# Attention log weights in three bf16 parts, one row for each head and chunk, in a fused conv, scan, attention and router kernel

## The chip, the cores and the metric

The kernel runs on one core of a Trainium2 chip, as one launch. The metric is device microseconds of that core, the median of several runs. Five engines work beside one another: TensorE (PE; its weight loads are listed as PEld), VectorE (DVE), ScalarE (ACT), GpSimd (POOL) and the sync engine (SP), which here only issues DMAs.

## The reference, cut to what matters

The input is `x` of 16 batches, 128 channels and 64 x 64 positions, so 4096 tokens a batch. Layer 0 is a group norm and a gated state-space scan (a short causal convolution, 256 inner channels, 16 states). Layer 1 is a layer norm, an attention without queries per token, and a router with 64 experts. The change lies in the attention:

```python
s = jnp.einsum('hd,bthd->bth', q_proj, k)          # 8 heads, one score a token
m_A = jax.lax.cummax(s, axis=1)                    # running maximum over the tokens
exp_scores = jnp.exp(s - m_A)
u_A = jnp.cumsum(exp_scores, axis=1)               # running sum: the denominator
w_A = jnp.cumsum(exp_scores[..., None] * v, axis=1)
output = w_A / u_A[..., None]
```

So the weight of token t in the output at token T is exp((s - m)[t] - log u[T]) for t up to T. `(s - m)` is called the log weight below, and `log u` the log denominator.

## The kernel before, in words

A batch is worked through in 8 blocks of L = 512 tokens, and a block in 4 chunks of P = 128 tokens; there are 128 blocks. The main loop (lines 624 to 800) handles in one turn `k` the scan of block `k` (`cur`), the end of the scan of the block before (`prev`), the preparation of the next block (`nxt`), and the attention of block `m = k - 9`, whose last two chunks are finished one turn later (`mp_`); the layer norm of the next attention block is `mn`. Turns 9 to 127, 119 of them, hold scan and attention; the first 9 hold no attention, the last 10 no scan. A turn has 16 steps `n`, one for each state of the scan.

A step does, on DVE, `product` (bx = du times B, into PSUM), then what `beside(n)` puts there, then `scan` for each half of the channels, with `between(n)` between the two halves; POOL multiplies the result by C (`da<-h,bct`) and keeps the last state; PE adds it up one or two steps later (`add_y`, y_ps). ACT makes the decays (`da<-delta,a_neg`) up to 8 steps ahead. B and C come by a DMA (bct, 512 KB, five buffers) that SP issues 3 steps ahead. Every engine's instructions stay in the order in which the program calls them (`InOrder`), so the list by step in `beside` and `between` is the order on each queue, SP's too. All eight PSUM banks are in use; three of them ("ps") rotate over most of the products.

The attention of block m, by steps: keys (0 to 2), scores (`score`, 1 and 3), running maximum and log weight on DVE (`score_max`, step 4, rows 64u + 32q + g of a head, 512 tokens in a row), the exponential (`score_exp`, 5), the running sum (`score_sum`, between the scans of step 6), logarithm and inverse (`score_log`, 7), the transposed first weights for the carried state (`turn_weights`, 8), values (8, 9, and 3 of the next turn), the matrix of weights (`weights`: 12 and 13, and 4 of the next turn), the products with the values (`attend`: 13, 14, and 5 and 6 of the next turn) and the carried state (`carry_on`, DVE: 14, 15, and 6 and 7 of the next turn).

`weights` builds the exponents of four heads at a time as an outer sum in PSUM: a bf16 product of identity and causal mask, then one f32 product of `lh[u]` (log weights as rows, and a row of -1) with `rh` (rows of ones, and the log denominators). The rows that hold data are filled by small DMAs from SBUF to SBUF on the SP queue: 4 of `lh` after step 4 (`spread_weights`) and 4 of `rh` after step 8 (`spread_log`).

The layer norm of the next attention block runs in steps 10 to 12: centre on PE, square on ACT, variance on PE after the two dt products, logarithm and exponential on ACT, and on DVE the product xn (`ln_apply`).

Of the kernel before, what the change touches and what calls it, by code (L numbers as in the profile page):

```python
# [39 lines left out]
def conv_attn_hybrid(ctx: ExitStack, tc: tile.TileContext, x, w_in, conv_w, conv_b, w_xproj, w_dt, b_dt,  # L40
# [4 lines left out]
    NBLK = T // L  # L45
    NCH = T // P
# [33 lines left out]
    with ExitStack() as st:  # L80
# [33 lines left out]
        q1 = wp.tile([P, 4, 2, 32], F32, name="q1")  # L114
        e1 = wp.tile([P, L // P * 4, 2, 32], F32, name="e1")
# [4 lines left out]
        lh = [wp.tile([P, L], F32, name=f"lh{u}") for u in range(2)]  # L120
        rh = wp.tile([P, 4, L], F32, name="rh")
        carry = wp.tile([P, L // P, P], F32, name="carry")
        negc = wp.tile([P, 1], F32, name="negc")
        nc.vector.memset(negc, NEG)
# [3 lines left out]
        for u in range(2):  # L128
            nc.vector.memset(lh[u], 0.0)
            nc.vector.memset(lh[u][64 * u : 64 * u + 32, :], -1.0)  # L130
            nc.vector.tensor_scalar(lh[u][64 * u : 64 * u + 32, :], lh[u][64 * u : 64 * u + 32, :],
                                    ident[64 * u : 64 * u + 32, 64 * u + 4 : 64 * u + 5], None, ALU.mult)
        nc.vector.memset(rh, 0.0)
        for x in range(4):
            nc.vector.tensor_copy(rh[:, x, :], bc(ident[:, x : x + 1], [P, L]))
        for x in range(4):
            nc.vector.tensor_copy(rh[64:, x, :], bc(ident[64:, 64 + x : 65 + x], [64, L]))
# [11 lines left out]
        with tc.tile_pool(name="prep", bufs=1) as prep:  # L149
# [15 lines left out]
            for g in range(2):  # L165
                nc.vector.tensor_copy(q1[:, :, g, g], qt_ps[:, 4 * g : 4 * g + 4])
# [115 lines left out]
        def store_bc(k):  # L282

            w = blocks[k]
            w["bcs"] = bcd.tile([2 * N, L], F32, tag="bcs", name="bcs")
            SP.dma_start(w["bcs"], w["dbl"][R:, :])
# [171 lines left out]
        def score(m, g):  # L458

            s = att[m]  # L460
            if g == 0:
                s["s"] = acc.tile([P, L], F32, tag="acc", name="s_ps")
            for j in range(4):
                PE.matmul(s["s"][32 * j : 32 * j + 32, :], q1[:, j, g, :], s.pop(("kt", 4 * g + j)),
                          start=(g == 0), stop=(g == 1))

        def score_max(m):
            b, i = divmod(m, NBLK)
            s = att[m]
            if i == 0:  # L470
                gn[b]["mx"] = stp.tile([P, 1], F32, tag="mx0", name="mx0")
                gn[b]["den"] = stp.tile([P, 1], F32, tag="den0", name="den0")
            s["e"] = a1.tile([P, L], F32, tag="e", name="e", bufs=2)
            mx = s["mx"] = a1.tile([P, L], F32, tag="mx", name="mx")
            DVE.tensor_tensor_scan(mx, bc(negc, [P, L]), s["s"], NEG if i == 0 else gn[b]["mx"], ALU.max, ALU.max)
            DVE.tensor_copy(gn[b]["mx"], mx[:, L - 1 : L])
            DVE.tensor_tensor(s["e"], s["s"], mx, ALU.subtract)

        def spread_weights(m):
            s = att[m]  # L480
            for u in range(2):
                for q in range(2):
                    r = 64 * u + 32 * q
                    SP.dma_start(lh[u][64 * u + 2 * q : 64 * u + 2 * q + 2, :], s["e"][r : r + 2, :])

        def score_exp(m):
            s = att[m]
            s["w"] = short("w")
            ACT.activation(s["w"], s["e"], AF.Exp)

        def score_sum(m):
            b, i = divmod(m, NBLK)
            s = att[m]
            DVE.tensor_tensor_scan(s["mx"], bc(ones[:, 0:1], [P, L]), s["w"], 0.0 if i == 0 else gn[b]["den"],
                                   ALU.mult, ALU.add)
            DVE.tensor_copy(gn[b]["den"], s["mx"][:, L - 1 : L])

        def turn_weights(m):
            s = att[m]
            et = bank("et_ps")  # L500
            w = s.pop("w")
            for c in range(L // P):
                PE.transpose(et[:, bass.ts(c, P)], w[:, bass.ts(c, P)], ident)
            etv = et.rearrange("p (n q) -> p n q", q=32)[:, :, 0:2]
            ACT.copy(e1.rearrange("p n g q -> p n (g q)")[:, :, 0::33], etv)

        def score_log(m):
            s = att[m]
            ACT.activation(s["mx"], s["mx"], AF.Ln)

            ACT.activation(s["e"], s["mx"], AF.Exp, scale=-1.0)

        def spread_log(m):
            s = att[m]
            mx = s.pop("mx")
            for u in range(2):
                for q in range(2):
                    r = 64 * u + 32 * q
                    SP.dma_start(rh[64 * u + 4 : 64 * u + 5, 2 * q : 2 * q + 2, :], mx[r : r + 2, :])
# [49 lines left out]
        def attend_before(m, c):  # L569
            s = att[m]  # L570
            if m % NBLK or c:
                PE.matmul(s["o"][:, bass.ts(c % 2, P)], carry[:, (c - 1) % 4, :], s["e"][:, bass.ts(c, P)], start=False,
# [51 lines left out]
        for k in range(NK + LAG + 1):  # L624
# [10 lines left out]
            def between(n):  # L635

                if n == 6 and m is not None:
                    score_sum(m)
# [3 lines left out]
            def beside(n):  # L642
# [60 lines left out]
                if n == 7:  # L703
                    if mp_ is not None:
                        attend_before(mp_, 3)
                    if nxt is not None:
                        conv(nxt, 1)
                    decays(k, n, 2)
                    if m is not None:
                        score_log(m)  # L710
# [4 lines left out]
                if n == 8:  # L715
# [5 lines left out]
                    if nxt is not None:  # L721
                        xproj(nxt)
                    if m is not None:
                        value(m, 0, 1)
                if n == 9:
                    if cur is not None:
# [3 lines left out]
                if n == 10:  # L730
                    if mn is not None:
                        ln_center(mn)
                        ln_square(mn)
                    if nxt is not None:
                        delta(nxt)
                    if mn is not None:
                        ln_var(mn)
                    load_exp()
                if n == 11:
# [355 lines left out]
```

## Time and profile before

| what | value |
|---|---|
| median of 3 runs | 10953.4 us (10951.26 to 10953.72) |
| profiled execution, its own time | 10953.32 us |
| span of the profiled execution | 10951.6 us |
| PE busy in the span | 9913.9 us, 91% |
| DVE busy | 9289.6 us, 85% |
| ACT busy | 6992.7 us, 64% |
| POOL busy | 7051.2 us, 64% |
| DMA queue of SP | 47.6% of 16 engines' time |

The share of an engine is an average over stages: turns without attention (to about 640 us), turns with scan and attention (to about 9694 us), attention alone (to about 10110 us), and then the router, the experts and the last sum. A window of eight turns with both shows what limits the kernel for five sixths of its time. In the tables an entry such as `w_ps<-rh,lh` names what is written and what is read; a f32 product appears as two records. [...] successive starts, not durations, give its price.

### The profile page before, as it was taken

What the parts mean: (1) busy time and instruction counts of PE and PEld (TensorE: products, weight loads), DVE (VectorE), ACT (ScalarE), POOL (GpSimd) and SP (SyncE); (2) the same over time, 40 slices, a digit from 0 to 9 for tenths busy, and PEclk for the clock granted to TensorE, in tenths of its full rate; (3) what the DMA queues carried; (4) which work ended last, traced back from release to release, by engine and by line L of the source; (5) the groups of instructions that cost most, each with busy time, mean ns of one, the idle gap of its engine ahead of it and who ended that gap; (6) DMA issues with size and microseconds to landing.
All of it is one profiled execution on the core that took longest, in us unless ns stands there. A gap on an engine that the chain in (4) does not pass through costs nothing.

```text
span 10951.6 us, 152501 instructions
## 1 busy us (share of the span) xinstructions
PE 9913.9 (91%) x54748; PEld 6015.7 (55%) x54748; DVE 9289.6 (85%) x9757; ACT 6992.7 (64%) x11244; POOL 7051.2 (64%) x3871
## 2 busy tenths in 40 slices
PE   6689999999999999999999999999999999999775
PEld 4455555555555555555555555555555555555752
DVE  8999998989989998999999898899899988941743
ACT  4566666666666666666666676666666666655640
POOL 6877776777777777777777777777777777730000
PEclk7789999999999999999999999999999999999886
DMA  5554445444454545444454445444444444421358
GB/s 145 139 148 131 143 131 147 126 138 136 132 146 125 148 128 146 131 134 139 129 145 128 144 133 140 131 137 138 138 136 130 140 132 142 125 67 34 109 160 335
DMA packets 772553, 1502.42 MB, mean 137 GB/s; under 512 B 58240, under 2 KB 127504, under 8 KB 764624
## 3 DMA queue, kind: packets, MB, share of 16 engines
q1 hardware_dynamic: 769744, 1492.13, 47.6%
q8 instruction: 430, 7.05, 0.3%
q14 instruction: 331, 2.71, 0.1%
q10 hardware_dynamic: 2048, 0.53, 0.0%
HBM read 1361.89 MB, written 126.35 MB: 136 GB/s over the span
## 4 chain that ended last, share of the span: by engine, by line
PE 57%; DVE 18%; ACT 11%; issue 6%; POOL 4%; DMA 3%; SPq 0%; POOLq 0%; DVEq 0%; ACTq 0%
PE y_ps L31 11%; DVE h L31 10%; PE v_ps L31 8%; PE xs_ps L31 8%; PE w_ps L31 6%; PE ao_ps L31 5%; DVE bx L31 5%; PE o_ps L31 4%; POOL da L31 4%; PE k_ps L31 3%; PE dbl_ps L31 2%; PE z_ps L31 2%; PE s_ps L31 2%; DVE du L31 2%; PE carry_ps L31 1%
## 5 line engine op out<-in xcount | busy, mean ns | idle before, releaser
L31 POOL TENSOR_TENSOR da<-h,bct 128x1024 f32<-128x1024 f32 x2048 | 6508.1, 3178 | 2649.4 <-DVE h L31 2216.1
L31 DVE TENSOR_TENSOR_SCAN h<-da,state,bx 128x512 f32<-128x512 f32 x3584 | 4405.5, 1266 | 105.5 <-DVE bx L31 3.3
L31 DVE TENSOR_TENSOR bx<-du,bct 128x1024 f32<-128x1024 f32 x2048 | 2680.7, 1309 | 191.6 <-DMA bct<-bcs 125.4
L31 PEld LDWEIGHTS y_ps<-ident,da 128*128 128x128 f32 x16384 | 1983.0, 147 | 1364.1 <-issue 693.5
L31 PE MATMUL y_ps<-ident,da 128*128 128x128 f32 x16384 | 2249.6, 286 | 492.8 <-POOL da L31 492.7
L31 ACT ACTIVATE da<-delta,a_neg 128x512 f32<-128x512 f32 x4096 | 2582.2, 712 | 0.2
L31 ACT ACTIVATE kt<-k_ps 128x512 f32<-128x512 f32 x1024 | 586.0, 602 | 979.6 <-PE k_ps L31 979.6
L31 ACT ACTIVATE v<-v_ps 128x512 f32<-128x512 f32 x1024 | 611.5, 599 | 795.9 <-PE v_ps L31 795.8
L31 PE MATMUL w_ps<-rh,lh 128*128 128x512 f32 x2048 | 1051.8, 595 | 0.4 <-DMA rh<-mx 0.4
L31 PE MATMUL k_ps<-xn,wk 128*128 128x512 f32 x2048 | 1019.3, 634 | 0.0
L31 PEld LDWEIGHTS ao_ps<-wm,v 128*128 128x128 f32 x8192 | 965.9, 192 | 69.3 <-issue 69.3
L31 PE MATMUL ao_ps<-wm,v 128*128 128x128 f32 x8192 | 999.1, 275 | 0.0
L31 PE MATMUL v_ps<-wv,xn 128*128 128x512 f32 x2048 | 986.2, 605 | 2.9 <-ACT xc L31 2.6
L31 PE MATMUL xs_ps<-xb,wc 128*128 128x512 f32 x2048 | 925.8, 594 | 1.8 <-issue 1.8
L31 ACT ACTIVATE wm<-w_ps 128x512 f32<-128x512 f32 x1024 | 583.8, 591 | 220.0 <-PE w_ps L31 214.1
L31 PEld LDWEIGHTS v_ps<-wv,xn 128*128 128x128 f32 x2048 | 358.4, 189 | 519.4 <-issue 492.9
L31 POOL COPY state<-h 128x2 f32<-128x2 f32 x1792 | 636.7, 355 | 0.0
L31 PEld LDWEIGHTS k_ps<-xn,wk 128*128 128x128 f32 x2048 | 385.3, 203 | 452.1 <-issue 402.4
L31 DVE TENSOR_TENSOR_SCAN h<-da,bx 128x512 f32<-128x512 f32 x512 | 598.6, 1206 | 16.1 <-DVE carry L31 0.3
L31 PEld LDWEIGHTS xs_ps<-xb,wc 128*128 128x128 f32 x2048 | 370.6, 191 | 373.1 <-issue 373.1
L31 PEld LDWEIGHTS w_ps<-rh,lh 128*128 128x128 f32 x2048 | 393.1, 192 | 258.0 <-issue 225.0
L31 ACT ACT_TABLE_LOAD x395 | 506.8, 1283 | 12.9 <-PE v_ps L31 5.9
(170 smaller groups left out, 9602.8 us busy)
## 6 DMA issues: line engine op xcount, KB each, us to landing
bct<-bcs SPq DMA_DIRECT2D x2048, 512.0 KB
xs<-t_d SPq DMA_DIRECT2D x256, 256.0 KB
xs<-in_x_dram SPq DMA_DIRECT2D x128, 256.0 KB
xt<-in_x_dram SPq DMA_DIRECT2D x64, 512.0 KB
t_d<-xt SPq DMA_DIRECT2D x64, 512.0 KB
t_d<-xs SPq DMA_DIRECT2D x256, 128.0 KB
t<-t_d SPq DMA_DIRECT2D x128, 256.0 KB
tc<-t_d SPq DMA_DIRECT2D x16, 2048.0 KB
```

What stands on the lines that cost most here:

```text
L31: return lambda *args, **kw: self.tc.keep_in_program_order(f(*args, **kw))
```

## The change

Scores. Each chunk of each head gets a row of its own: `score` makes 16 products of 32 x 128 instead of 4 of 32 x 512 for each group, so a score tile has 128 columns, and rows 5g + c of each quadrant hold head group g, chunk c. Running maximum and sum scan 128 columns in each row, and `from_chunks` joins the four chunks of a head: a 32 x 32 block transpose on DVE of the last 32 columns, a copy of two numbers from the state of the block before (`zs`, two alternating tiles), two scans of 4 numbers, a transpose back. The log weight is then one scalar_tensor_tensor.

Log weight and log denominator lie beside each other in one tile (`x2`, 2 x 128 columns). ACT writes its bf16 rounding (first part), DVE the rest in two further bf16 parts (`split_more`, between the scans of step 8). The parts go to DRAM by one DMA (`store_parts`, after step 8) and come back by 16 DMAs of 3 rows each, 8 of `lh` and 8 of `rh` (`spread_parts`, after step 10). `lh` and `rh` are bf16, so the product in `weights` is bf16. The 8 small DMAs of before are gone. The running sum's logarithm takes the sum of the chunks before as bias; the inverse is made by four exponentials, one for each chunk, with a bias that switches the other rows off.

Order. The centre and square of the layer norm move from step 10 to the head of step 9, its variance ahead of the dt products, its logarithm and exponential from step 11 to 10, xn from step 12 to 13; `load_x(mn)` from step 8 to 7; `store_bc` from the SP queue to the ACT queue, right after xproj. `score_log` is called ahead of the decays of step 7.

```diff
+        q1 = wp.tile([P, 4, 2, CB, 32], F32, name="q1")
+        lh = [wp.tile([P, L], BF16, name=f"lh{u}") for u in range(2)]
+        rh = wp.tile([P, 4, L], BF16, name="rh")
...
-            SP.dma_start(w["bcs"], w["dbl"][R:, :])
+            ACT.dma_start(w["bcs"], w["dbl"][R:, :])
...
+            kt = [s.pop(("kt", 4 * g + j)) for j in range(4)]
+            for c in range(CB):
+                for j in range(4):
+                    PE.matmul(s["s"][32 * j : 32 * j + 32, :P], q1[:, j, g, c, :], kt[j][:, bass.ts(c, P)],
+                              start=(g == 0 and c == 0), stop=(g == 1 and c == CB - 1))
+
+        def from_chunks(m, what, local, first, op0, op1, data):
+            b, i = divmod(m, NBLK)
+            last = stp.tile([P, 32], F32, tag=f"last_{what}", name=f"last_{what}")
+            DVE.transpose(last, local[:, P - 32 :])
+            z = zs[what][m % 2]
+            if i == 0:
+                DVE.memset(z[:, 0:10:5], first)
+            else:
+                DVE.tensor_copy(z[:, 0:10:5], gn[b][what][:, 4:14:5])
+            gn[b][what] = z
+            for g in range(2):
+                DVE.tensor_tensor_scan(z[:, 5 * g + 1 : 5 * g + 5], bc(data[:, 0:1], [P, CB]),
+                                       last[:, 5 * g : 5 * g + 4], z[:, 5 * g : 5 * g + 1], op0, op1)
+            back = stp.tile([P, 32], F32, tag=f"back_{what}", name=f"back_{what}")
+            DVE.transpose(back, z)
+            return back[:, 31:32]
...
-            DVE.tensor_tensor_scan(mx, bc(negc, [P, L]), s["s"], NEG if i == 0 else gn[b]["mx"], ALU.max, ALU.max)
-            DVE.tensor_copy(gn[b]["mx"], mx[:, L - 1 : L])
-            DVE.tensor_tensor(s["e"], s["s"], mx, ALU.subtract)
+            DVE.tensor_tensor_scan(s["mx"], bc(negc, [P, P]), s["s"][:, :P], NEG, ALU.max, ALU.max)
+        def score_less(m):
+            before = from_chunks(m, "max", mx, NEG, ALU.max, ALU.max, negc)
+            DVE.scalar_tensor_tensor(x[:, 0, :], mx, before, s["s"][:, :P], ALU.max, ALU.subtract)
...
-            ACT.activation(s["w"], s["e"], AF.Exp)
+            ACT.activation(s["w"], s["x2"][:, 0, :], AF.Exp, scale=-1.0)
...
-            DVE.tensor_tensor_scan(s["mx"], bc(ones[:, 0:1], [P, L]), s["w"], 0.0 if i == 0 else gn[b]["den"],
-                                   ALU.mult, ALU.add)
-            DVE.tensor_copy(gn[b]["den"], s["mx"][:, L - 1 : L])
+            DVE.tensor_tensor_scan(s["sum"], bc(ones[:, 0:1], [P, P]), s["w"], 0.0, ALU.mult, ALU.add)
+            s["before"] = from_chunks(m, "sum", s["sum"], 0.0, ALU.mult, ALU.add, ones)
...
-            for c in range(L // P):
-                PE.transpose(et[:, bass.ts(c, P)], w[:, bass.ts(c, P)], ident)
+            PE.transpose(et[:, :P], s.pop("w"), ident)
+            for g in range(2):
+                ACT.copy(dst[:, :, :, g, 5 * g : 5 * g + 4],
+                         bc(src[:, 5 * g : 5 * g + 4, :].unsqueeze(3), [P, CB, 4, CB]))
...
-            ACT.activation(s["mx"], s["mx"], AF.Ln)
-            ACT.activation(s["e"], s["mx"], AF.Exp, scale=-1.0)
+            ACT.activation(x[:, 1, :], s.pop("sum"), AF.Ln, bias=s.pop("before"))
+            s["parts"] = a1.tile([P, 3, 2, P], BF16, tag="parts", name="parts")
+            ACT.copy(s["parts"][:, 0], x)
+        def inverse(m):
+            for c in range(CB):
+                ACT.activation(s["e"][:, c, :], s["x2"][:, 1, :], AF.Exp, bias=off[:, c : c + 1], scale=-1.0)
+        def split_more(m):
+            DVE.tensor_tensor(x, x, parts[:, 0], ALU.subtract)
+            DVE.tensor_copy(parts[:, 1], x)
+            DVE.tensor_tensor(parts[:, 2], x, parts[:, 1], ALU.subtract)
+        def store_parts(m):
+            s["pd"] = bcd.tile([P, 3, 2, P], BF16, tag="pd", name="pd")
+            SP.dma_start(s["pd"], s.pop("parts"))
+        def spread_parts(m):
             for u in range(2):
-                for q in range(2):
-                    r = 64 * u + 32 * q
-                    SP.dma_start(rh[64 * u + 4 : 64 * u + 5, 2 * q : 2 * q + 2, :], mx[r : r + 2, :])
+                for x in range(4):
+                    r = 64 * u + 32 * (x // 2) + 5 * (x % 2)
+                    SP.dma_start(lh[u][64 * u + 3 * x : 64 * u + 3 * x + 3, :].rearrange("t (c s) -> t c s", s=P),
+                                 pd[:, 0, r : r + CB, :])
+                    SP.dma_start(rh[64 * u + 12 : 64 * u + 15, x, :].rearrange("t (c s) -> t c s", s=P),
+                                 pd[:, 1, r : r + CB, :])
...
-                if n == 6 and m is not None:
-                    score_sum(m)
+                if m is not None:
+                    if n == 4:
+                        score_less(m)
+                    if n == 6:
+                        score_sum(m)
+                    if n == 8:
+                        split_more(m)
...
-                if n == 4 and m is not None:
-                    spread_weights(m)
...
                 if n == 8 and m is not None:
-                    spread_log(m)
-                if n == 8 and nxt is not None:
-                    store_bc(nxt)
+                    store_parts(m)
+                if n == 10 and m is not None:
+                    spread_parts(m)
```

The constant tiles are built differently too, once at the start: `lh` and `rh` hold -1 or +1 in the rows that no DMA fills, `off` is a small new constant, and `q1` has the form that the scores need.

## The prediction

> **What bounds the kernel now.** I read the page's busy line first, then a window of eight turns that hold both scan and attention, the waits in it, the order of single instructions in one turn, and the groups that the change touches.
>
> ```profile
> 4949.00:5558.00 609.00, 572.24 (x3147) 344.05 (x3147) 550.46 (x519) 413.00 (x650) 439.47 (x241) 0.98 0.48 136
> ```
>
> The columns are window, length, busy time of PE, PEld, DVE, ACT, POOL, then PE clock, DMA share, GB/s. A turn takes 609 / 8 = 76.1 us; the stretch from about 640 to 9694 us gives 9054 / 119 = 76.1 too. PE is busy 71.5 us of it, DVE 68.8, ACT 51.6, POOL 54.9. Two engines are near the bound, neither at it, so the waits decide.
>
> ```profile
> DVE xn L31 <- ACT rstd L31: 19.8, 8, 2.9
> DVE bx L31 <- DMA bct<-bcs: 10.0, 8, 1.8
> DVE xs L31 <- PE ao_ps L31: 7.0, 7, 1.1
> DVE carry L31 <- PE carry_ps L31: 6.7, 6, 1.6
> ```
>
> These are DVE's waits in that window: us, times, longest. Per turn 2.5 us for xn, 1.25 for the B and C transfer, 0.9 and 0.8 for products of PE, with small ones 46.7 / 8 = 5.8 us. So DVE waits for PE in steps 6 to 8, and in step 12 for a chain PE, ACT, DVE. The chain of waits says the same: in 5000 to 5200 us it lies on PE from step 1 to 10, then on ACT (square, table, delta, table, rstd) and then on DVE until POOL's last product.
>
> ```profile
> 5102.19 2.45 DVE L31 TENSOR_TENSOR_SCAN h<-da,state,bx 128x512 f32<-128x512 f32 x2
> 5105.68 2.62 DVE L31 TENSOR_TENSOR bx<-du,bct 128x1024 f32<-128x1024 f32 x1 [1.04 <-DMA bct<-bcs]
> 5110.74 0.69 DVE L31 TENSOR_TENSOR xn<-cen_ps,rstd 128x512 f32<-128x512 f32 x1 [2.44 <-ACT rstd L31]
> ```
>
> DVE in order of time, start and duration first: step 12. bx comes late, after POOL's product has begun (4.87), and takes 2.62 instead of 1.23 us. Then xn waits.
>
> ```profile
> 5070.77 0.38 PE L31 MATMUL w_ps<-maskb,identb 128*128 128x512 bf16 x1
> 5070.99 1.02 PE L31 MATMUL w_ps<-rh,lh 128*128 128x512 f32 x2
> 5071.85 0.38 PE L31 MATMUL w_ps<-maskb,identb 128*128 128x512 bf16 x1
> ```
>
> PE in order of time. By starts, a bf16 product of 512 columns costs 0.22 us and the f32 one 0.86.
>
> ```profile
> L31 DVE TENSOR_TENSOR_SCAN mx<-ones,den,w 128x512 f32<-128x512 f32 x112 | 195.9, 1749 | 0.0
> L31 DVE TENSOR_TENSOR_SCAN mx<-negc,mx,s_ps 128x512 f32<-128x512 f32 x112 | 142.6, 1273 | 65.8 <-PE s_ps L31 65.8
> L31 DVE TENSOR_TENSOR gs<-mv,gs 128x1 f32<-128x1 f32 x16 | 21.9, 1368 | 0.6
> L31 SPq DMA_DIRECT2D lh<-e x512: 562/575/702, 654.0 to 10076.0; - x171
> L31 SPq DMA_DIRECT2D bct<-bcs x2048: 355/360/2113, 42.7 to 9680.2; - x187
> ```
>
> Groups: busy us, mean ns (the SP rows: ns min/median/max). The same scan costs 0.48 us more with both inputs in SBUF, and a product of one element takes 1.37 us in the mean where it takes 0.16 alone: POOL holds them up. A small DMA of two rows occupies SP for 0.575 us, a large one for 0.36.
>
> [...]
>
> **The change, part by part (per turn).** I count DVE by starts. A plain step (bx, two scans) goes from 5058.30 to 5062.15: 3.85; 16 of them 61.6. On top: z 0.96, two xs 0.2, stats and du 1.9, xn 0.45, the carries about 0 (they fit in the gap before the scan), the maximum 1.75 (step 4: 5.60), the sum 1.45 or 2.10 (POOL in the way), mean 1.8. Sum 68.7; with 5.8 of waits and 1.4 of the doubled bx 75.9, against 76.1.
>
> DVE, removed: 1.75 + 1.8 = 3.55, leaving 65.15. Added:
> - Step 4. A scan of 128 columns, 1.27 / 4 plus a fixed part, so 0.38, half of it in the gap before the scan: 0.2. Then two transposes (0.155, the smallest instruction here, [...] I take 0.2), a copy 0.1, two scans of 4 numbers 0.19 and 0.15 (dependent tiny instructions start 0.19 apart in the group norm: 26.25, 26.44, 26.63), the last operation about 0.3 (the carry's 128x128 row: 0.28). 1.3 together. POOL's product still runs about 0.4 when the first two-input scan comes. 1.7.
> - Step 6. Scan 0.38, POOL in the way 0.75 (the 1.98 of one sum scan less 1.26), the rest as above without the last: 0.83. 1.95.
> - Step 8. Two products of 256 elements ([...]), a cast 0.25 (0.21 for 128 columns at the start of the trace) and gaps: 1.1, and 0.4 of POOL. 1.5.
>
> 65.15 + 5.15 = 70.3. Bounds: 1.2 less if POOL is never in the way and transposes cost 0.155; 2.5 more if every dependent instruction costs 0.35 and POOL 0.8 each time.
>
> PE, removed: 8 products, 0.86 to 0.22, 5.1 us; three of four transposes, 0.33. Added: 0.15 per score group (32 records of 32 x 128 at the carry's 0.57 per 16, 1.14 against 0.99), 0.3. So 71.5 falls to 66.3. Half of the 5.1 lies in steps 4 and 5, ahead of the carries and xs for which DVE waits; the other half in steps 12 and 13.
>
> Waits. xn: 2.5 now. Square before the gates and variance before dt bring rstd forward by about 2 us, xn itself is a step later: 0.3 left. A wait of about 1 us moves to the second dt product, which needs the bank of the first (as var waits now, 0.8). The transfer's 1.25 and the doubled bx 1.4 go, because SP no longer waits for dbl ahead of it (SP waits 31.0 us in the window for that): 0. xs and carries: PE comes 2.6 us earlier, DVE about as much since it doesn't wait any more; 0.6 and 0.5 left. At the turn of a batch 0.4.
>
> The sixteen DMAs. They stand on SP behind bct of step 13, which needs POOL's product of step 8. Counted from bx of step 8: split done at 4.6, parts stored by about 7 (at the start of the trace bcs is issued at 41.01 and the first bct, which waits for it, at 42.67: 1.7 us), bct issued at 9.4 to 9.8, 16 x 0.57 (three rows taken like two) = 9.1, so the last is issued at 18.9 and lands about 21. PE reaches weights(m, 0) at about 21.4: y of step 15 at 38, then 53.7 us of products, less 70.3. Behind it wait y of step 10, attend(0) and the carry that DVE wants at about 26.5; ready about 26.6. Behind the sixteen on SP stand xb and the bct of step 14, issued at 19.7; its 257 and 512 KB, at the 5.6 us that one needed behind two loads in step 12, land at about 25.3, wanted at 25.9. So the sixteen cost nothing up to 0.57 each, and nearly 16 times any excess. I put 0.5 of waits.
>
> ACT: exp, log, inverse and copy of 512 columns (0.62 + 0.62 + 0.63 + 0.22) give way to 0.31 + 0.31, four of 0.31, a copy 0.41, two of 0.25 and an issue of about 0.4 (as for o_d on ACT's queue): plus 1.1. It has 24 us free in a turn, which hide it; without that cover 1.1 x 119 = 131 us. POOL has no new work. load_x one step earlier costs nothing, its tile being free.
>
> Sum: 70.3 + 0.3 + 0.6 + 0.5 + 0.4 + 0.5 = 72.6. 76.1 - 72.6 = 3.5, times 119 = 416 us. The ten turns without scan: PE saves 5.1 of 44.1, but now nothing hides store, sixteen DMAs and landing (about 14 us from split to weights): 0, within 20 us either way. Turns without attention: 0. The start: about 1 us more of DVE constants. 10953.3 - 416 + 1 = 10538 us; the profiled execution stands 0.1 us from the median, so 10540.
>
> **Rivals.**
> 1. Slower: the sixteen DMAs become the bound. An issue above 0.82 us each uses up the gain (72.6 + 16 x 0.25 - 0.5 = 76.1); so would landings 4 us later. At 1.0 us, 79 us a turn and 11300. For it: they are all in one place, on one queue, between a late producer and two consumers with half a microsecond to spare; each has three rows of four pieces of 256 bytes. Against: nothing in the trace above 0.70 for a small DMA that didn't wait.
> 2. DVE becomes the bound at a higher price: small dependent instructions and POOL take 2.5 us more, 75.1 a turn, 10835. For it: the 1.37 us of a one-element product.
> 3. DVE's waits vanish altogether and small ones are cheap: 70 a turn, 10230. Against: PE at 66.3 plus its own waits is close behind.
> 4. No change: PE's relief is worthless because DVE's added work equals its waits. Needs 5.8 us more on DVE than removed; I find 1.6.
>
> **How the numbers follow.** Mine: 62%, 71.5 to 73.8 a turn, 10405 to 10680. Rival 2: 11%. Rival 3, all below 10405: 10%. Rival 1: 11% slower, and 3% where it eats most of the gain. Rival 4: 3%. A difference of 0.2%, 22 us, is about what a measurement can tell. Faster 0.62 + 0.11 + 0.10 + 0.03 = 0.86, same 0.03, slower 0.11. To hold 8 in 10 the range takes rival 2, the edge of 3 and the mild form of 1: 10380 to 10900.
>
> **What would show it.** w_ps as one bf16 record, PE busy near 66 a turn; xn's wait on rstd under 0.5; no bct wait in step 12; DVE near 70 with the scans of sum and the split stretched by POOL; `lh<-pd` near 0.57 each; no wait of w_ps on DMA. I am wrong if w_ps waits for `rh<-pd` by more than 2 us, if bx of step 14 waits for bct, or if the small DVE instructions sum to over 7 us.

## The result, and the profile after

The changed kernel takes 10682.4 us (median of 4 runs, 10670.12 to 10698.19); the kernel before, beside it on the same chip, 10953.6 us. The ratio is 0.9753, 95% interval 0.9736 to 0.977: 271 us, 2.5%, are gained. The prediction was 10540 within 10380 to 10900. The sign and the range are right; of the 416 us that the sum promised for the main stage, 249 came.

The profiled execution took 10670.12 us, its span is 10668.4 us. The main stage, from the first turn with attention to the last with a scan, went from 9060 us (647.1 to 9707.05) to 8811 us (643.9 to 9455.0): 74.0 us a turn in place of 76.1. The attention-only turns after it take 20 us less (402 to 382, to the last `xs`), the router and the experts behind them 11 us less, and the start 3 us less.

Eight turns with both scan and attention, the columns as in the window shown for before (window, length, busy PE, PEld, DVE, ACT, POOL, clock, DMA share, GB/s):

```profile
4798.10:5389.80 591.70, 541.56 (x3439) 336.32 (x3437) 553.26 (x609) 416.21 (x690) 436.00 (x242) 0.97 0.52 143
```

PE is busy 67.7 us a turn (71.5 before), DVE 69.2 (68.8), ACT 52.0 and POOL 54.5. DVE's waits in that window (us, times, longest):

```profile
DVE carry L31 <- PE carry_ps L31: 11.8, 7, 2.1
DVE xt L31 <- DMA xt<-in_x_dram: 6.8, 1, 6.8
DVE xn L31 <- ACT rstd L31: 3.4, 4, 1.1
DVE xs L31 <- PE ao_ps L31: 1.5, 2, 1.0
```

xn's wait fell from 2.5 to 0.43 us a turn, and the wait of bx for its transfer is gone. But the carry's wait rose from 0.8 to 1.5, and a wait for the residual input (`xt<-in_x_dram`) has grown from 0.2 to 6.8 us, in one place: the turn with the residual.

What the carry waits for, in one turn. First ACT, then PE, in order of time (start, duration):

```profile
4921.76 2.55 ACT L31 ACTIVATE da<-delta,a_neg 128x512 f32<-128x512 f32 x4
4924.21 1.06 ACT L31 ACTIVATE wm<-w_ps 128x512 f32<-128x512 f32 x2
```

```profile
4917.00 1.46 PE L31 MATMUL dt_ps<-dbl,wdt 8*128 8x512 f32 x2 [0.78 <-ACT delta L31]
4918.39 3.25 PE L31 MATMUL y_ps<-ident,da 128*128 128x128 f32 x16
...
4921.69 0.38 PE L31 MATMUL w_ps<-rh,lh 128*128 128x512 bf16 x1
...
4924.84 0.38 PE L31 MATMUL w_ps<-maskb,identb 128*128 128x512 bf16 x1 [1.03 <-ACT wm L31]
4925.27 1.95 PE L31 MATMUL ao_ps<-wm,v 128*128 128x128 f32 x16
4927.15 0.65 PE L31 MATMUL carry_ps<-v,e 128*32 128x128 f32 x16
```

The bf16 product makes exponents ready at about 4922. ACT, in its written order, does four decays first and takes the exponential only at 4924.2. PE stands for 1.03 us until a bank is free, and the products behind it, the carry's among them, come later. The 16 products of y_ps ahead of the weights took 3.25 us, where 16 of the same took 1.97 at 4931.37: the granted clock of TensorE was 0.83 from 4915 to 4919 us, 0.74 from 4919 to 4923 and 1.00 in the next 4 us. More on that below.

Before, the wait between PE and ACT ran mostly the other way: ACT waited for the f32 products. The same pair over the whole span, of before and then of after:

```profile
ACT wm L31 <- PE w_ps L31: 214.1, 444, 3.5
```

```profile
ACT wm L31 <- PE w_ps L31: 46.6, 39, 8.2
...
PE w_ps L31 <- ACT wm L31: 161.2, 215, 1.6
```

The groups that the change touches (busy us, mean ns | idle before it; SP rows: ns min/median/max):

```profile
L31 PE MATMUL w_ps<-rh,lh 128*128 128x512 bf16 x1024 | 410.3, 401 | 52.3 <-DMA rh<-pd 52.0
L31 DVE TENSOR_TENSOR bx<-du,bct 128x1024 f32<-128x1024 f32 x2048 | 2524.5, 1233 | 72.8 <-DMA bct<-bcs 2.7
L31 DVE TENSOR_TENSOR_SCAN sum<-ones,w 128x128 f32<-128x128 f32 x128 | 144.6, 1130 | 0.0
L31 DVE TENSOR_TENSOR x<-x,parts 128x256 f32<-128x256 f32 x128 | 102.3, 799 | 0.5
```

```profile
L31 SPq DMA_DIRECT2D lh<-pd x1024: 232/276/1077, 676.7 to 9812.7; - x171
```

`w_ps<-rh,lh` is one bf16 record. bx has its plain 1.233 us again (1.309 in the mean before). The sum's scan (1.13 us in the mean) and the first operation of the split (0.80) are stretched: with POOL's product out of the way they took 0.42 and 0.40 (at 4755.99 and 4767.91, in the kernel with PE's cost back, see below). A small DMA occupies SP for 0.276 us, not 0.57.

### The profile page after: what moved, and what is told of

It reads as the page before. It is cut to its first block, busy times and chain, and to the rows that moved or that the text cites. A ratio compares the mean times of both kernels' runs of the same rounds, so it can differ in the third digit from the quotient of the medians.

```text
span 10668.4 us, 165082 instructions
## 1 busy us (share of the span) xinstructions
PE 9433.2 (88%) x59484; PEld 5912.8 (55%) x59484; DVE 9296.3 (87%) x11184; ACT 7034.1 (66%) x11884; POOL 6977.9 (65%) x3875
## 4 chain that ended last, share of the span: by engine, by line
PE 56%; DVE 16%; ACT 15%; issue 5%; POOL 4%; DMA 4%; SPq 1%; POOLq 0%; ACTq 0%; DVEq 0%
PE y_ps L31 10%; DVE h L31 8%; PE v_ps L31 8%; PE xs_ps L31 7%; PE ao_ps L31 7%; PE k_ps L31 4%; POOL da L31 4%; PE o_ps L31 4%; DVE bx L31 3%; ACT L208 2%; PE dt_ps L31 2%; ACT da L31 2%; PE carry_ps L31 2%; PE dbl_ps L31 2%; PE w_ps L31 2%
## 5 line engine op out<-in xcount | busy, mean ns | idle before, releaser
L31 POOL TENSOR_TENSOR da<-h,bct 128x1024 f32<-128x1024 f32 x2048 | 6597.9, 3222 | 2470.7 <-DVE h L31 1524.4
L31 DVE TENSOR_TENSOR_SCAN h<-da,state,bx 128x512 f32<-128x512 f32 x3584 | 4424.3, 1266 | 101.5 <-DVE bx L31 2.8
L31 PEld LDWEIGHTS y_ps<-ident,da 128*128 128x128 f32 x16384 | 2057.4, 152 | 1318.9 <-POOL da L31 652.6
L31 PE MATMUL y_ps<-ident,da 128*128 128x128 f32 x16384 | 2347.5, 294 | 485.3 <-POOL da L31 485.1
L31 ACT ACTIVATE da<-delta,a_neg 128x512 f32<-128x512 f32 x4096 | 2606.8, 722 | 0.2
L31 DVE TENSOR_TENSOR bx<-du,bct 128x1024 f32<-128x1024 f32 x2048 | 2524.5, 1233 | 72.8 <-DMA bct<-bcs 2.7
L31 ACT ACTIVATE kt<-k_ps 128x512 f32<-128x512 f32 x1024 | 586.6, 602 | 862.8 <-PE k_ps L31 858.1
L31 ACT ACTIVATE v<-v_ps 128x512 f32<-128x512 f32 x1024 | 611.6, 599 | 795.3 <-PE v_ps L31 795.2
L31 PE MATMUL k_ps<-xn,wk 128*128 128x512 f32 x2048 | 1047.1, 648 | 0.0
L31 PE MATMUL v_ps<-wv,xn 128*128 128x512 f32 x2048 | 1000.2, 611 | 6.3 <-ACT xc L31 6.0
L31 PE MATMUL ao_ps<-wm,v 128*128 128x128 f32 x8192 | 1003.1, 276 | 0.0
L31 PEld LDWEIGHTS ao_ps<-wm,v 128*128 128x128 f32 x8192 | 971.2, 193 | 25.6 <-issue 6.2
L31 PE MATMUL xs_ps<-xb,wc 128*128 128x512 f32 x2048 | 924.3, 594 | 1.8 <-issue 1.8
L31 DVE TENSOR_TENSOR_SCAN h<-da,bx 128x512 f32<-128x512 f32 x512 | 601.2, 1207 | 15.4 <-DVE bx L31 0.5
L31 PEld LDWEIGHTS v_ps<-wv,xn 128*128 128x128 f32 x2048 | 338.7, 189 | 475.0 <-issue 308.7
L31 PEld LDWEIGHTS k_ps<-xn,wk 128*128 128x128 f32 x2048 | 389.9, 206 | 377.4 <-issue 346.5
L31 PE MATMUL w_ps<-maskb,identb 128*128 128x512 bf16 x1024 | 411.5, 402 | 187.4 <-ACT wm L31 161.2
L31 PEld LDWEIGHTS xs_ps<-xb,wc 128*128 128x128 f32 x2048 | 370.0, 191 | 372.1 <-issue 372.1
L31 ACT ACTIVATE wm<-w_ps 128x512 f32<-128x512 f32 x1024 | 539.4, 594 | 48.2 <-PE w_ps L31 46.6
L31 POOL COPY state<-h 128x2 f32<-128x2 f32 x1792 | 472.8, 264 | 0.0
L31 PE MATMUL w_ps<-rh,lh 128*128 128x512 bf16 x1024 | 410.3, 401 | 52.3 <-DMA rh<-pd 52.0
```

The costliest lines, as they stand in the source:

```text
L31: return lambda *args, **kw: self.tc.keep_in_program_order(f(*args, **kw))
```

## The experiments

The theory to which the runs led: DVE's work plus DVE's waits add up to the time, but don't set it; PE and what PE waits for set the pace of the turn, so PE's 5 us are the gain, and two waits that the new schedule made (ACT's exponential behind the decays, the residual behind the sixteen DMAs) take part of it back. It was not the theory at the start: of the first four expectations, those for the order alone and the rows alone still count DVE's waits as gains, that for the run without the split calls DVE the bound, and all four, PE's cost back among them, missed with their own ranges. The rivals: the order of the layer norm and of the store of B and C is the gain; DVE's added work is what took the rest; the sixteen DMAs did.

All ratios are against the kernel before, run beside the kernel. The differences in us below are of medians; taken by the ratios they change by about 8 us at most.

| kernel | us | ratio, 95% |
|---|---|---|
| after | 10682.4 | 0.9753 (0.9736 to 0.977) |
| before + new order alone | 11023.1 | 1.0072 (1.0057 to 1.0087) |
| new rows and parts, old order | 10781.0 | 0.985 (0.9836 to 0.9865) |
| after + PE's cost back | 11092.5 | 1.0131 (1.0114 to 1.0148) |
| after, no split on DVE | 10662.9 | 0.9739 (0.9724 to 0.9753) |
| before + store of B and C on ACT | 10949.0 | 0.9992 (0.9984 to 1.0001) |
| after + decays a step later | 10533.3 | 0.9622 (0.9607 to 0.9636) |
| after + residual earlier | 10609.4 | 0.9691 (0.9677 to 0.9706) |
| after + both | 10455.1 | 0.9553 (0.9537 to 0.9569) |
| both, no split on DVE | 10427.7 | 0.9522 (0.9507 to 0.9536) |
| after, each small DMA twice | 11820.9 | 1.0799 (1.0783 to 1.0815) |
| after + sixteen other small DMAs | 10928.1 | 0.9977 (0.9968 to 0.9985) |

### Order alone, and rows alone

The kernel before with only the moves of the order (f32 rows and products as they were):

```diff
                 if n == 9:
+                    if mn is not None:
+                        ln_center(mn)
+                        ln_square(mn)
...
                 if n == 10:
-                    if mn is not None:
-                        ln_center(mn)
-                        ln_square(mn)
+                    if mn is not None:
+                        ln_var(mn)
                     if nxt is not None:
                         delta(nxt)
-                    if mn is not None:
-                        ln_var(mn)
                     load_exp()
-                if n == 11:
                     if mn is not None:
                         ln_scale(mn)
                 if n == 12:
-                    if mn is not None:
-                        ln_apply(mn)
                     if m is not None:
                         weights(m, 0)
                 if n == 13:
+                    if mn is not None:
+                        ln_apply(mn)
...
-            SP.dma_start(w["bcs"], w["dbl"][R:, :])
+            ACT.dma_start(w["bcs"], w["dbl"][R:, :])
```

(`store_bc` right after xproj, and `load_x(mn)` in step 7, belong to it.) The second kernel is the changed one with these edits taken back.

> The kernel before with the moves of order alone: the layer norm's centre and square at the head of step 9, variance ahead of dt, xn in step 13, load_x in step 7, bcs issued on ACT's queue; scores, log weights and the f32 product in weights stay as they were. My theory (PE's products and the order each had to go): DVE loses its waits for rstd (2.5 us a turn), for bct (1.25) and the doubled bx (1.4), but PE still has 71.5 us of work and its waits, so a turn falls from 76.1 to about 74.5: 10760 us, between 10690 and 10850. Rival A (the order is the whole gain): a turn of 74.1 and 10680 within 30. Rival B (PE's shorter product is the whole gain): 10950 within 30.

> The changed kernel with the old order: rows of a head and a chunk, three bf16 parts and the bf16 product, but the layer norm in steps 10 to 12 as before, load_x in step 8, bcs on SP after step 8 (behind the store of the parts). My theory: DVE's waits for PE in steps 6 to 8 go (1.7 us a turn), those for rstd and bct stay (5.1), and DVE's own work is 1.6 more: about 76 a turn, 10940 us, between 10850 and 11020. Rival A (the order is the whole gain): the same or slower, 10950 to 11150, since only DVE's added work is left. Rival B (the product is the whole gain): 10700 within 40.

Order alone: 11023.1, slower by 0.7%; rows alone: 10781.0. All the numbers expected for the two missed, those of the rivals too. DVE's waits with the order alone:

```profile
DVE carry L31 <- PE carry_ps L31: 710.9, 327, 10.8
DVE xn L31 <- ACT rstd L31: 346.4, 122, 9.7
```

Before, the carry waited 271.9 us in all and xn 387.3. The wait of bx for its transfer is all but gone here too (5.3 us left of 125.4), and it bought nothing: 439 us more of waiting stand at the carry. Read as a square, by the ratios and 10953 us: the rows alone give 0.0150, or 164 us; with f32 rows the new order costs 0.0072, or 79 us, and with bf16 rows it gains 0.985 - 0.9753, or 106 us. The order only pays once PE has become shorter. So "the order is the gain" falls, and so does a sum in which each part has a value of its own.

PE itself became slower with the order alone. Busy time and number of instructions, of before and then with the order alone:

```profile
PE 9913.9 (91%) x54748; PEld 6015.7 (55%) x54748; DVE 9289.6 (85%) x9757; ACT 6992.7 (64%) x11244; POOL 7051.2 (64%) x3871
PE 10058.7 (91%) x54748; PEld 6074.6 (55%) x54748; DVE 9102.6 (83%) x9757; ACT 6994.6 (63%) x11244; POOL 6998.0 (63%) x3871
```

The same products kept PE busy for 145 us more, and the mean granted clock fell from 0.948 to 0.939. Much of it lies behind the layer norm's products: in the 10 us from the first dt product of a turn the clock was 0.95 in the mean of 118 turns before, 0.87 with the order alone and 0.86 in the changed kernel. The store of B and C alone (below) left PE's busy time at 9908.6 and the clock at 0.949, so the slower PE came with the moves of the layer norm and of `load_x`. How much of the 79 us this makes up, and what lowers the clock there, no run shows.

### PE's cost back, and DVE's cost of the split away

To the changed kernel, three products with a zero weight for each product of `weights` give PE back what bf16 saved, in cost and not in value:

```diff
+                for _ in range(3):
+                    PE.matmul(rp, zero, rh[:, :, bass.ts(c, P)], start=False, stop=False)
                 PE.matmul(rp, lh[u][:, bass.ts(c, P)], rh[:, :, bass.ts(c, P)],
                           start=False, stop=True)
```

The other kernel leaves out the split on DVE in step 8 (second and third part are zeros):

```diff
-                    if n == 8:
-                        split_more(m)
```

> The changed kernel with PE's saving given back and nothing else: each bf16 product in weights is followed in the same sum by three more of the same shape with an all-zero weight matrix, so four bf16 products take the time of the f32 one (4 x 0.22 us against 0.86), the sum is unchanged, and PE has 5.1 us more a turn. My theory: PE is then at 71.5 plus 3 us of waits, a turn at 75.5 to 76.5: 10850 to 10970 us. Rival A (PE had slack all along): within 40 us of 10682.

> The changed kernel without the split on DVE: the second and third parts stay zero, so the log weights and log denominators are only bf16 precise; the 17 DMAs and all else stay. It takes 1.7 us of DVE a turn away (0.80 + 0.29 + 0.43 and gaps, of which 0.4 to 0.6 is POOL in the way). My theory (DVE is the bound now, PE close behind): DVE would gain 1.7 but PE lets it have only part, about 0.8 a turn: 10590 us, between 10500 and 10650. Rival (PE, not DVE, is the bound now, as the carry's wait in step 14 suggests): within 40 us of 10682.

PE's cost back: 11092.5, 410 us over the changed kernel, or 3.45 us a turn for some 5.1 us of PE (24 products of 0.21 us by starts). It is slower than before, and beyond the 10850 to 10970 that were expected. It differs from the order alone only by the rows and parts, at the same busy time of PE (10062.1 us and 10058.7), and is 0.6% slower. So the change, put together in this order, has three parts: the order costs 0.7% of the time of before, the rows and parts with their DMAs 0.6%, and the shorter product on PE gains 3.8%.

DVE's split away: 10662.9, 20 us for 1.7 us a turn of DVE, which would be 200 us if DVE set the pace. The expected 10500 to 10650 was missed; the rival's number, within 40 us of the changed kernel, came. DVE's waits without the split:

```profile
DVE carry L31 <- PE carry_ps L31: 359.5, 144, 15.2
DVE xn L31 <- ACT rstd L31: 279.9, 119, 11.3
```

xn waited 118.1 us in the changed kernel: 162 of the 200 us became waiting for the layer norm. Time that DVE saves there turns into a wait. PE's time counts at about two thirds (3.45 of 5.1).

### The store of B and C on ACT's queue, alone

```diff
-            SP.dma_start(w["bcs"], w["dbl"][R:, :])
+            ACT.dma_start(w["bcs"], w["dbl"][R:, :])
```

(called right after xproj instead of after step 8; the kernel before otherwise)

> The kernel before with one edit: the store of B and C goes from SP's queue (after step 8) to ACT's queue, right after xproj. If PE sets the pace, the 1.25 us a turn that bx of step 12 waits for the transfer, and the 1.4 us by which POOL doubles its time, move to other waits of DVE (xn, carries), and the time stays: 10910 to 10960. Rival, my prediction's sum, in which DVE's time and waits add up to the turn: 1.25 to 2.65 us a turn, 10630 to 10800.

10949.0, a ratio of 0.9992: no change, as the theory of PE had it. DVE lost most of its wait for the transfer (125.4 us in all, 18.0 left) and 136 us of work, the doubled bx (9289.6 to 9153.5 us). What it waits for now:

```profile
DVE xn L31 <- ACT rstd L31: 629.6, 126, 11.9
DVE carry L31 <- PE carry_ps L31: 273.1, 131, 10.8
```

xn waits 242 us more than before. In the prediction this edit was counted as 1.25 + 1.4 us a turn.

### The two new waits removed

Decays of the next steps start one step later, so that ACT takes the exponential of `weights(m, 0)` first; the residual's four loads are issued four steps earlier, ahead of the sixteen DMAs on SP:

```diff
-                    if 4 <= n <= 6 or n >= 11:
+                    if 4 <= n <= 6 or n >= 12:
```

```diff
-                if 8 <= n <= 11 and i == 1 and cur is not None:
-                    load_residual(b, n - 8)
+                if 4 <= n <= 7 and i == 1 and cur is not None:
+                    load_residual(b, n - 4)
```

> The changed kernel with one call of decays fewer: those of step 11 move to the steps 12 to 15, so that ACT takes up the exponential of the weights of chunk 0 right after rstd instead of behind four decays (2.55 us). My theory of the carry's wait in step 14 (1.45 to 2.1 us in every turn): PE's fourth mask product waits 1.0 to 1.6 us for a bank that ACT empties late, because the product is now shorter than ACT's exponential and ACT stands behind the decays. Then the wait of w_ps on ACT wm goes, the carry's falls below 0.8, and about 1 us a turn is won: 10570 us, between 10520 and 10640. Rival (the carry is late because PE reaches step 12 late, its dt product waiting for delta): w_ps no longer waits but the carry still does by over 1.2, within 40 us of 10682.

> The changed kernel with the four loads of a batch's residual issued after steps 4 to 7 of its second turn instead of 8 to 11, ahead of the sixteen small DMAs. In the window of eight turns DVE waits 6.8 us for xt once (0.2 before the change), in a turn of 77 to 78 us. My theory (the last part of the residual stands on SP behind the sixteen): the wait goes, these 15 or 16 turns fall by 4 to 6 us, 10610 us, between 10580 and 10640. Rival (the 2 MB themselves take that time, whenever they are issued, and hold up bct): 10682 within 25.

> The two edits together, on the changed kernel: decays of step 11 later, residual loads after steps 4 to 7. They touch different waits, so their gains should add: about 10500 us, between 10440 and 10590. If only one of them holds, 10570 to 10610.

10533.3 (149 us less), 10609.4 (73 less), and both 10455.1 (227 less; the sum of the two is 222), each within its expected range. With both, ordinary turns went from about 72 to 74 us to about 70.5 to 72, and the turn with the residual from about 77.6 to 73. DVE's and PE's waits with the decays a step later:

```profile
DVE carry L31 <- PE carry_ps L31: 237.3, 99, 14.6
```

```profile
PE w_ps L31 <- ACT wm L31: 63.5, 128, 1.3
```

PE's wait for ACT's exponential fell from 161.2 to 63.5 us, the carry's from 360.7 to 237.3 (between 1000 and 9000 us, where every turn has scan and attention, from 158.8 to 46.4). Part of the gain shows in PE itself: for the same number of products its busy time fell from 9433.2 us to 9366.4 with the decays later and to 9315.9 with both, at a mean granted clock of 0.931, 0.934 and 0.941. The runs don't part this from the waits. The version with both leaves none of the work out; it is 2.1% faster than the changed kernel, 4.5% faster than the one before.

> The kernel with both repairs (decays a step later, residual four steps earlier) and without DVE's three operations of the split in step 8: the second and third part are zeros, so 1.7 us a turn of DVE's work are left out. In the kernel after leaving them out was worth 20 us. If the repairs have made DVE the bound, it is worth most of 1.7 x 119 = 200 us now: 10455 less 120 to 200, 10255 to 10335. If PE still sets the pace, within 40 us of 10455. Between: both, 10335 to 10415.

With both repairs and without the split (the edit shown above): 10427.7, 27 us less than 10455.1. That is within the 40 us expected if PE still sets the pace, so DVE's operations in step 8 are still not on the path. Only that place was tried; nothing here says what DVE's time is worth in other steps.

### The price of the small DMAs

First each of the sixteen DMAs was issued twice; then sixteen more went behind the sixteen, to a tile that nobody reads:

```diff
+            for y in range(16):
+                SP.dma_start(spare[8 * y : 8 * y + 3, :].rearrange("t (c s) -> t c s", s=P), pd[:, 0, y : y + CB - 1, :])
```

> The changed kernel with each of the sixteen small DMAs issued twice, the same bytes to the same place: 32, at 0.28 us each (measured median) 5 us more of SP in steps 10 to 12. My prediction said that the sixteen cost nothing up to a threshold and then nearly their excess: with the last issued at 17.7 us after bx of step 8 and needed by PE at 22, some 2 us are free, so 2 to 3 us a turn are lost, in the waits of w_ps for rh<-pd and in the carry: 10990 us, between 10880 and 11100. Rival (the landings are hidden well beyond that): within 40 us of 10682.

> The kernel after, with sixteen more small DMAs from the stored parts into a tile that nobody reads (three rows of three pieces of 256 bytes each), issued behind the sixteen in pairs with them, ahead of what stands behind them on SP. No data is changed. A clean price of a longer burst, since no two neighbours have one destination. By the kernel after an issue takes 0.276 us: 16 more are 4.4 us, so xb and the transfer of step 14 are issued 4.4 us later (22.1 us after bx of step 8 in place of 17.7) and land at about 27.7, wanted at 25.9. My prediction's threshold (slack about 0.5 us at a last issue of 18.9, so about 1.7 us at 17.7) then charges 4.4 - 1.7 = 2.7 us a turn, some part of it taken back by waits that are there anyway: 10682 + 119 x (1.5 to 2.7), 10860 to 11000, and bx waits for bct by 1.5 to 2.7 us a turn. Rival: the burst is hidden with far more room than I saw; then within 40 us of 10682 and no bct wait.

Twice: 11820.9, 1138 us or 9.6 a turn, far above what was expected. It is no clean price: SP issued four and then stood for about 1 us, again and again, and its own waits name the landing of the first DMA to the same place, 8 times a turn:

```profile
SPq L31 <- DMA lh<-pd: 1084.5, 1024, 4.9
```

This wait is not among those of the changed kernel. The run also shows who stands behind a late burst:

```profile
PE w_ps L31 <- DMA rh<-pd: 1150.7, 128, 17.4
...
DVE bx L31 <- DMA bct<-bcs: 987.9, 108, 11.7
```

Sixteen others: 10928.1, 246 us or 2.07 a turn, within the 1.5 to 2.7 expected. bx waits 330.4 us for bct (2.7 before the edit), 2.75 more a turn, a little above what was expected. One turn, SP and then DVE; bx of step 8 began at 5024.89:

```profile
5042.26 5.37 SPq L31 DMA_DIRECT2D spare<-pd  x16
...
5048.19 0.89 SPq L31 DMA_DIRECT2D bct<-bcs  x2
```

```profile
5053.64 1.23 DVE L31 TENSOR_TENSOR bx<-du,bct 128x1024 f32<-128x1024 f32 x1 [3.22 <-DMA bct<-bcs]
```

The sixteen extra take 5.4 us of SP (0.34 each with the gaps). The transfer of step 14 is issued 23.3 us after bx of step 8 and used 5.45 us later, at 28.75, where it was wanted at 25.5. The prediction had 5.6 from issue to landing and 25.9: about right. In the changed kernel it is issued at 18.2 (4917.64 less 4899.41), so about 1.9 us of room are left there (an estimate: 25.5 less 18.2 and 5.45). This also bounds the word "PE sets the pace": of the 2.75 us that DVE waits more, 2.07 lengthen the turn, so at step 14 DVE has less than a microsecond to spare, and what it loses there goes on to POOL and to PE's y (`PE y_ps L31 <- POOL da L31`: 485.1 us in the changed kernel, 654.9 here).

## Why the prediction was right in sign and too large in size

**The step that failed.** "Sum 68.7; with 5.8 of waits and 1.4 of the doubled bx 75.9, against 76.1", used as an account from which each removed wait is gained. It balances, since DVE is always either working or waiting, but that is so on any engine and doesn't make DVE the one that sets the pace. Of the 2.65 us of bct wait and doubled bx, the run with the store alone got nothing; of 1.7 us of DVE's work, the run without the split got 0.17. PE's 5.1 us, which the prediction booked only as 0.6 less of waiting for xs and the carries (1.7 to 1.1), are what the time responds to, with 3.45. The chain of waits on the page of before, which the prediction read for one stretch only, has it over the whole span:

```profile
PE 57%; DVE 18%; ACT 11%; issue 6%; POOL 4%; DMA 3%; SPq 0%; POOLq 0%; DVEq 0%; ACTq 0%
```

PE's products make up 57% of the chain that ended last, DVE 18% (56% and 16% after the change). A term of DVE's should have been weighed by where in the turn it stands, not counted in full.

**Why the number still fell in the range.** DVE must wait for PE or the other way round, so a right forecast of DVE's work and waits gives the right turn, whatever sets the pace. The prediction had 70.3 of work and 2.3 of waits; measured, 3.1 of waits and so 70.8 for the rest, 74.0 us in the window in place of 72.6. That the total came so near is in part luck, since its parts, run alone, are worth something else: what was booked in full gave nothing, and what was booked at 0.6 gave 3.45. Term by term:

| term, us a turn | predicted | measured |
|---|---|---|
| DVE added in step 4 / 6 / 8 | 1.7 / 1.95 / 1.5 | 1.90 / 2.05 / 1.90 (5.73, 5.88, 5.73 less a plain step of 3.83; the last with one xs of about 0.1) |
| DVE by starts, the sum | 70.3 | 70.8 (the turn less the listed waits) |
| PE busy | 66.3 | 67.7 (68.2 from 1000 to 9000 us) |
| xn's wait | 0.3 | 0.43 |
| xs | 0.6 | 0.19 |
| carries | 0.5 | 1.5 |
| batch turn (with the residual) | 0.4 | 0.85 |
| bct of step 14 | 0.5 | 0 |
| attention-only turns, in all | 0 within 20 | -20 |
| start | +1 | -3 |

In the first row, the prediction's 1.1 for the split without POOL's share and 0.2 for a transpose were its author's estimates. Measured, the three operations of the split took 0.41 (the 41 of the first that POOL's product doesn't overlap), 0.29 and 0.43, and the transposes 0.19 to 0.21.

The mis-sized term is the carry: "PE comes 2.6 us earlier, DVE about as much since it doesn't wait any more; 0.6 and 0.5 left." In the turn that the prediction shows and in the one shown above, both counted from bx of step 8, PE ends the carry's product at 29.8 us and then at 28.4, 1.4 earlier; DVE is ready for it at 30.7 and then at 26.8, 3.9 earlier. PE starts on `weights(m, 0)` at about 22.1 in both. Its shorter products save 2.6 us there, and the wait for ACT, whose queue holds the exponential behind four decays, takes 1.03 of it back; the turn of before has no such wait. The prediction followed PE's and SP's queues past the moved work and counted only the time of ACT ("It has 24 us free in a turn, which hide it"), not its order. The decays a step later gave 149 us back, the residual 73 us: together 227, more than the 167 us that were missing (416 less 249), so that with both repairs the kernel is below the forecast.

PE's own term was mis-sized too, 66.3 where 67.7 came. The prediction put the moved wait at the second dt product at no cost. The wait is as long as it was (91.8 us in 118 times at var before, 92.7 in 119 at dt after), but in the turn shown the products behind it run at a lower clock. Between 1000 and 9000 us the granted clock was 0.98 before and 0.96 after; 0.02 of 74 us is 1.5 us a turn, an estimate, of the 1.9 by which PE's term is off over that stretch.

The other new wait is the residual: the prediction asked what stands behind the sixteen on SP, and named xb and the bct of step 14. In one turn of eight the last load of the residual stands there too, and it was put down as "At the turn of a batch 0.4".

**Right.** The order of the layer norm brought rstd forward as said, and no bx waits in step 12. The sum and the split were stretched by POOL's product about as said. The cheapest place to see it is the new copy of two numbers, first in step 4, then in step 6:

```profile
4952.98 3.25 POOL L31 TENSOR_TENSOR da<-h,bct 128x1024 f32<-128x1024 f32 x1 [1.43 <-DVE h L31]
4955.54 0.72 DVE L31 COPY z_max<-z_max 128x2 f32<-128x2 f32 x1
```

```profile
4965.75 0.32 POOL L31 COPY state<-h 128x2 f32<-128x2 f32 x1
4966.26 0.13 DVE L31 COPY z_sum<-z_sum 128x2 f32<-128x2 f32 x1
```

POOL's product ends at 4956.23 and the copy of the maximum at 4956.26; the copy of the sum finds POOL idle. It is so in the whole trace: the 104 copies of the maximum that overlap POOL's product end 0.02 to 0.03 us after it and take 0.72 us in the mean, the 8 that don't 0.127, like all 112 of the sum. The sum's scan took 1.18 us in the mean where the product overlaps it (119 times) and 0.42 where not (9 times), the first operation of the split 1.00 (85) and 0.41 (41). Not every operation of DVE is held so: the transpose of the last columns of the maximum (`last_max<-mx`) took 0.186 beside the same product (119 times). What makes the difference is not shown. ACT's added work had its cover. Rival 1 was not this kernel's case, but its mechanism is real: sixteen more issues put the time at 0.9977 of before.

**Right by luck.** The burst was put at 16 x 0.57 = 9.1 us. Each took 0.276 (0.32 from start to start); the burst still lasted 8.0 us (4909.08 to 4917.08), because SP paused for 2.6 us inside it. SP's own waits from 4910.8 to 4913.7 us hold one entry, the landing of a transfer of B and C:

```profile
SPq L31 <- DMA bct<-bcs: 2.6, 1, 2.6
```

Over the whole span this wait of SP is 280.4 us, 32.9 before the change. Why one of the small DMAs has to wait for that landing stays open. The 0.57 for each was the prediction's estimate, three rows taken like the two of before (0.575 from SBUF to SBUF); that few rows make an issue dear is not borne out by 3 rows from DRAM to SBUF, at 0.276.

**Rivals.** 2 (DVE dearer) had 0.7 us of its 2.5, and falls as the bound as far as step 8 goes, by the run without the split; what was added in steps 4 and 6 was not left out in any run. 3 falls with a turn of 74 us, 4 with a gain of 2.5%.

**Open.** Of the 106 us that the order gains with bf16 rows, the runs don't say which move brings it: the store alone brought nothing in the kernel before, and the moves of the layer norm were not run alone. What lowers TensorE's clock behind the dt products, and how much of each time it is, was not tested. Nor was the residual's or the decays' move tried in the kernel before.

## What to carry to other kernels

An account that balances on one engine says where its time goes, not that the engine sets the pace: before a removed wait is booked as a gain, ask whether the engine would meet the same wait a little later, and look at each engine's share of the chain of waits, here 57% against 18%. When one engine gets faster, look for the pair of waits that will turn round, here PE and ACT around the exponential, and move what stands ahead on the other engine's queue; that was worth half as much as the change itself. Compare an engine's busy time and clock for the same instructions before and after a change of order: here PE took 145 us more for the same products. What is issued behind a new burst of DMAs has to be listed for every kind of turn, also for the one that comes once in eight.

## What was not expected of the hardware

- A DMA of 3 rows (12 pieces of 256 bytes) from DRAM to SBUF occupies SP for 0.276 us, one of 2 rows from SBUF to SBUF for 0.575, one of B and C for all partitions 0.36.
- Two small DMAs to the same place don't follow one another at the price of the issue: SP waited for the landing of the first, 1.06 us each time in the mean (1084.5 us in 1024 waits), and sixteen doubled ones cost 9.6 us a turn where sixteen others cost 2.07. Whether the program's own order of two writes or the hardware holds them was not told apart.
- The granted clock of TensorE changes within a turn and with the order of the instructions: 0.95, 0.86 and 0.92 in the mean of the 10 us from the first dt product, before, after and with both repairs. 16 products of y_ps took 1.91 us before (5108.48) and 3.25 after (4918.39), both just behind a wait of 0.78 us for delta.
- A copy of 2 numbers in each partition takes 0.127 us, or 0.72 in the mean where POOL's product still runs (0.680 over all 112 copies of the maximum); the first operation of the split 1.05 us in the median where it still runs, or 0.40 where the product had ended before it (in the kernel with PE's cost back).
